# Every second wide mask on GpSimd, and ten checks at the end in thirds of a row

## The chip, the cores and the metric

The kernel runs on one core of a Trainium2 chip. Its engines work in parallel, each through its own list of instructions in a fixed order: TensorE (PE, matrix products), VectorE (DVE), ScalarE (ACT), GpSimd (POOL), and SyncE (SP), which here only starts transfers. They meet through semaphores. The metric is the device time of one execution in microseconds (us), as the median of several runs; the profile is of one further execution.

## What is computed

Four graph layers on a feature table `x` of 2708 nodes by 128 features, with one adjacency matrix `adj` of 2708 x 2708:

```python
_a = bernoulli(..., 0.00295421, (2708, 2708)); adj = _a / max(_a.sum(-1), 1)
for layer in (0, 1, 2, 3):
    h = maximum(layernorm(x), 0)
    x = x + layer(h, adj)
# layer 0: hyperbolic aggregation; layer 1: gelu messages summed over neighbours;
# layer 2: relu(adj @ (h @ W2));   layer 3: h @ W_self + (adj @ h / deg) @ W_neigh
```

A row of `adj` has some eight entries that are not zero, and all of them in a row have the same value, 1 over their number.

## The kernel before, in words

The nodes are cut into 22 tiles of 128 rows (the last has 20), and the tiles into six blocks of four (the last of two). The kernel reads `adj` transposed once, and keeps it on the chip as `mask`, one byte an element, 1 where an entry is not zero. With `mask` a product with the adjacency is a product of features with ones and zeros, and the value of each row, `val`, is multiplied in afterwards. For layer 1 it lists the neighbours of each row and gathers their feature rows from DRAM with indirect transfers, which POOL issues, tile after tile.

The work has four stretches:

- the opening (0 to about 150 us): mask, neighbour lists, layer 0;
- the loop (to about 404 us): POOL gathers, tile after tile; `messages` adds, activates and sums the gathered rows, `update` and `update_one` form the new rows of `x` and split them in three bf16 parts, and `share` multiplies the parts with the mask (layer 2's product, L2820). In gaps of the loop stand the checks of `check_part` (L2846);
- the drain after the last gather (404 to about 426 us): the last tiles' messages and updates, and the last `share`;
- the endgame (to the end): layer 2 is finished block by block (`take_two`, `times_w2`, then `one_of` for the four tiles of block 0 and `layer_two` for the other blocks), and each block's normalised rows `h` are split into a pair of fp32r parts: a rounded part by ACT (L3091, L3159) and a remainder by DVE (L3071, L3148). Layer 3's product with the adjacency is `three` (L3032): for each tile t, two parts by six blocks, twelve matmuls. Its mask operand must be fp32r too, so `widen` (L2428) copies the tile's mask, 2708 elements a row, from one byte to four, into one of five buffers; tile t uses the buffer that tile t-5 used, so it waits until that tile is multiplied (`multiplied`). Meanwhile `third_own` forms `h @ W_self` (L3176, L3180, L3185, L3200). The last five tiles are multiplied block by block, so that a block can be taken (L3318), multiplied by `W_neigh` (L997), scaled (L3325), added (L3330) and stored (L3333) while PE does the next.

The checks: that all entries of a row are one value isn't taken on trust. For every row the kernel reads `adj` again, as it lies in DRAM, counts the elements that equal `val` and later compares the count with `deg` (`wrong_rows`, L3246). If any row differs, a flag leads to a second, dense program that stands behind this one. The rows of tiles 0 to 15 (`CHECKS = 16`) are checked in the loop, in thirds of 904 columns: SP fetches, DVE compares into bytes (L2862), ACT sums (L2868). Those of tiles 16 to 21 are checked in the endgame by `check` (L3206), in halves of 1354 columns: SP fetches a whole row of the tile into one of two buffers (L3213), DVE compares and sums in one instruction (L3218).

The order of all this is written by a planner in the kernel itself (L788 to L914). Each step is entered by `op(engine, took, step, after, due, ring, filler)` with an estimated duration, the steps that it follows, a due time and, where it takes a buffer of a ring, which one; a `filler` gives way to other steps of its engine until it is due. `carry_out` then plays the plan through with these estimates and writes the instructions of each engine in the order that comes out. On the chip the order is fixed; what really takes longer than planned delays all that stands behind it on its engine.

Two points of the plan matter here. `begun_wide` (L2947) opens the first two buffers of the wide masks, so masks 0 and 1 can be made before the loop has ended. `turned` (L2981) closes the memory of the loop and opens that of the endgame; all other buffers (rows of the checks, the other masks, the pairs) exist only after it.

Of the kernel before, what the change touches and what calls it, by code (L numbers as in the profile page):

```python
# [29 lines left out]
F32 = mybir.dt.float32  # L30
# [12 lines left out]
P = 128  # L43
# [18 lines left out]
LAG = 3  # L62
WIDE = 5
MID = 1354.0
CHECKS = 16


def dense_stack(
# [491 lines left out]
def sparse_stack(  # L560
# [30 lines left out]
    def rows(t):  # L591
        return min(P, N - t * P)
# [1830 lines left out]
    wide_one, wide_mask = [], {}  # L2423

    def widening(t, after, due):
        return op("ACT", 2.47, lambda: widen(t), after, due, filler=True)

    def widen(t):  # L2428

        pool = wide_one[0] if t % WIDE < 2 else wide_one[1]  # L2430
        m = pool.tile([P, N], F32R, tag=f"wm{t % WIDE}", name=f"wm{t}")
        nc.scalar.copy(m, mask[:, t, :])  # L2432
# [4 lines left out]
    middle = -(-N // 2)  # L2437
    middle += middle % 2
    sides = ((0, middle), (middle, N))
    nb = len(blocks)  # L2440
    assert T == 22 and nb == 6 and rest

# [517 lines left out]
    def turn():  # L2960

        st_m.close()
        held.close()

        def pool(name, bufs):
            made[name] = st.enter_context(
                tc.tile_pool(name=name, bufs=bufs, reuse_waits="tile")
            )
            return made[name]

        pool("group2", 2)
        pool("block2", 2)
        wide = pool("wide2", 1)
        pool("eq", 1)
        pool("rows", 2)
        wide_one.append(pool("widemask", 1))
        made["pair"] = wide.tile([P, T, 2, D], F32R, name="pair")
        for name in ("rdeg", "clipped", "wrong", "some"):
            made[name] = wide.tile([P, T], F32, name=name)
# [223 lines left out]
        frees(s, k)  # L3203
        return k

    def check(t, due):  # L3206

        n = rows(t)
        my = {}

        def fetch():
            my["row"] = made["rows"].tile([P, N], F32, tag="row", name=f"row{t}")
            nc.sync.dma_start(out=my["row"][:n, :], in_=adj[t * P : t * P + n, :])  # L3213

        def equal(k):
            c0, c1 = sides[k]
            eq = made["eq"].tile([P, middle], F8, tag="eq", name=f"eq{t}_{k}")
            nc.vector.tensor_scalar(  # L3218
                eq[:n, : c1 - c0],
                my["row"][:n, c0:c1],  # L3220
                val[:n, t : t + 1],
                None,
                op0=ALU.is_equal,
                op1=ALU.add,
                accum_out=same[:n, t, k : k + 1],
                saturate=False,
            )

        f = op("SP", 0.1, fetch, [turned], due - 15.0, ring=("rows", 2))
        e = [  # L3230
            op("DVE", 1.65, lambda k=k: equal(k), [(f, 8.0), parts_begun], due + 1.6 * k,
               filler=True)
            for k in range(2)
        ]
        frees(f, *e)
        return e

    def inverse():
        rdeg, clipped = made["rdeg"], made["clipped"]
# [164 lines left out]
```

## Time and profile before

| | |
|---|---|
| median of 3 runs | 623.64 us (617.2 to 625.9) |
| the profiled execution, its own time | 522.63 us |
| its span, first to last instruction | 520.9 us |
| busy: PE, DVE, ACT, POOL | 431.5, 405.6, 349.4, 216.3 us |
| mean granted clock of PE | 0.90 |
| wide masks on ACT (L2432), 22 | 53.0 us busy, 2446 ns each |
| checks in the loop: DVE L2862, ACT L2868, 48 each | 685 ns (median) and 946 ns each |
| checks in the endgame: DVE L3218, 12 | 1622 ns each (median) |
| gathers on POOL in the loop (L2467) | 72 and 65, 1004 and 1032 ns each |
| POOL after the last gather, from 404.8 us | nothing |

The time of the profiled execution is its own, taken in the same way as the others; it is some 101 us below the median of the timed runs, and nothing in the profile tells why. Sums below are made against the profiled execution. A share of busy time is a mean over stretches with different limits, so each stretch is looked at by itself. In a row of groups the columns are line, engine, operation, what it writes and reads with shapes, count, busy us and mean ns, and idle time of the engine before them with what ended it. A row of the timeline has start, duration, engine, line, operation. In the chain of waits each row is start, duration and what the end of the program waited for at that moment.

### The profile page before, as it was taken

How to read it: one execution, taken by the hardware profiler on the slowest of the kernel's cores; microseconds unless marked ns; L12 is line 12 of the kernel's file. 1: busy time of each engine (PE TensorE's matmuls, PEld its weight loads, DVE VectorE, ACT ScalarE, POOL GpSimd, SP SyncE). 2: the span in 40 equal slices, each digit the busy share in tenths (PEclk: the TensorE clock that was granted, in tenths of full speed). 3: DMA queues.
4: the chain of work that ended last, by engine and by line, in shares of the span. 5: the costliest groups of instructions: out<-in, count | busy, mean ns of one | idle time of the engine just before them, and what ended most of it. 6: DMA issues, size and time to landing. Idle time of an engine off the chain costs nothing.

```text
span 520.9 us, 8318 instructions
## 1 busy us (share of the span) xinstructions
PE 431.5 (83%) x2442; PEld 295.3 (57%) x2442; DVE 405.6 (78%) x1740; ACT 349.4 (67%) x746; POOL 216.3 (42%) x270
## 2 busy tenths in 40 slices
PE   0787899999999699816789878897886898999793
PEld 0674354556557566615555646554554446888583
DVE  6888954879955895589978897999886879999432
ACT  2738965789823173465656678989787878999910
POOL 8800000000047777667777777777777000000000
PEclk9999799999999655767579997999997999999898
DMA  8893189992151111311222387769877341160012
GB/s 255 287 312 94 72 305 342 319 361 73 32 143 55 52 47 54 96 37 50 85 54 53 86 264 224 222 202 292 268 229 227 120 162 54 46 270 23 1 52 64
DMA packets 41942, 77.89 MB, mean 150 GB/s; under 512 B 5418, under 2 KB 18278, under 8 KB 41226
## 3 DMA queue, kind: packets, MB, share of 16 engines
q1 hardware_dynamic: 33582, 63.15, 35.9%
q0 software_dynamic: 6560, 13.38, 10.2%
q10 hardware_dynamic: 1744, 0.72, 0.5%
q8 instruction: 21, 0.34, 0.3%
q14 instruction: 35, 0.29, 0.2%
HBM read 73.62 MB, written 3.62 MB: 148 GB/s over the span
## 4 chain that ended last, share of the span: by engine, by line
DVE 41%; PE 23%; ACT 16%; DMA 12%; issue 6%; POOL 1%; ACTq 0%; DVEq 0%
DMA a<-in_adj_t_dram 7%; DVE eq L3218 3%; PE acc L2085 3%; PE three L3032 3%; ACT wm L2432 3%; DVE eq L2862 3%; ACT mask L1482 3%; PE u L1429 2%; ACT eq L2868 2%; DMA layer_w<-in_L_gnn_layer_dram 2%; PE msg L2535 2%; PE own L997 2%; PE own L1005 2%; PE two L2820 1%; DVE r_all L1108 1%
## 5 line engine op out<-in xcount | busy, mean ns | idle before, releaser
L2344 POOL DMA_INDIRECT early<-d_early,early_c x42 | 41.6, 990 | 134.9 <-DVE wt L1732 122.4
L2467 POOL DMA_INDIRECT g<-d_hbm,head_c x72 | 72.3, 1004 | 26.7 <-issue 16.2
L2467 POOL DMA_INDIRECT gt<-d_hbm,tail_c x65 | 67.1, 1032 | 19.8 <-issue 14.9
L2820 PE MATMUL two<-mask,parts 128*128 128x512 fp8e4 (+1 forms) x288 | 64.3, 360 | 3.3 <-ACT parts L2739 3.1
L3032 PE MATMUL three<-wm,pair 128*128 128x512 f32 (+1 forms) x264 | 62.4, 386 | 2.0 <-ACT pair L3091 1.3
L2085 PE MATMUL acc<-mask,parts 128*128 128x512 fp8e4 (+1 forms) x288 | 59.8, 362 | 2.7 <-ACT parts L1653 1.8
L3032 PEld LDWEIGHTS three<-wm,pair 128*128 128x128 f32 x264 | 47.3, 194 | 11.6 <-ACT pair L3091 1.7
L2432 ACT CAST wm<-mask 128x2708 fp32r<-128x2708 fp8e4 x22 | 53.0, 2446 | 0.0
L2868 ACT ACTIVATE eq<-eq 128x904 fp8e4<-128x904 fp8e4 (+1 forms) x48 | 45.4, 946 | 5.7 <-DVE eq L2862 5.5
L1482 ACT ACTIVATE mask<-a 128x2048 fp8e4<-128x2048 uint32 (+5 forms) x32 | 40.3, 1294 | 12.3 <-DMA a<-in_adj_t_dram 12.3
L2085 PEld LDWEIGHTS <-parts 128*128 128x128 bf16 x288 | 27.1, 100 | 32.0 <-ACT parts L1653 2.3
L2820 PEld LDWEIGHTS <-parts 128*128 128x128 bf16 x288 | 27.6, 100 | 26.8 <-ACT parts L2739 3.8
L2535 PE MATMUL msg<-rt,gt 128*128 128x128 f32 x130 | 23.1, 321 | 15.9 <-ACT gt L2613 15.7
L2535 PEld LDWEIGHTS msg<-rt,gt 128*128 128x128 f32 x130 | 19.2, 219 | 22.2 <-ACT gt L2613 21.8
L1678 PE MATMUL pk<-mask,shifts 128*128 128x512 fp8e4 (+1 forms) x132 | 28.8, 354 | 1.9 <-ACT mask L1482 1.9
L2529 PE MATMUL msg<-ident,g 128*128 128x128 f32 x144 | 25.0, 322 | 5.0 <-ACT g L2594 3.6
L2529 PEld LDWEIGHTS msg<-ident,g 128*128 128x128 f32 x144 | 21.1, 223 | 8.3 <-ACT g L2594 6.3
L2820 PE MATMUL two<-mask,partsh 128*128 128x512 fp8e4 (+1 forms) x108 | 23.3, 361 | 2.4 <-ACT partsh L2739 1.7
L2497 PEld LDWEIGHTS <-r_all 128*128 128x128 fp8e4 x195 | 15.3, 111 | 16.7 <-issue 15.3
L2497 PE MATMUL msg<-parts,r_all 128*128 128x128 bf16 x144 | 13.5, 253 | 12.3 <-DVE v L1031 10.5
L2085 PE MATMUL acc<-mask,partsh 128*128 128x512 fp8e4 (+1 forms) x108 | 21.9, 354 | 0.0
L1678 PEld LDWEIGHTS <-shifts 128*128 128x128 bf16 x132 | 12.5, 101 | 12.7 <-issue 2.0
(472 smaller groups left out, 1054.9 us busy)
## 6 DMA issues: line engine op xcount, KB each, us to landing
a<-in_adj_t_dram SPq DMA_DIRECT2D x25, 1024.0 KB
early<-in_adj_dram SPq DMA_DIRECT2D x16, 452.0 KB
hT<-in_adj_dram SPq DMA_DIRECT2D x16, 452.0 KB
row<-in_adj_dram SPq DMA_DIRECT2D x5, 1354.0 KB
early<-in_adj_dram SPq DMA_DIRECT2D x8, 450.0 KB
hT<-in_adj_dram SPq DMA_DIRECT2D x8, 450.0 KB
a<-in_adj_t_dram SPq DMA_DIRECT2D x5, 296.0 KB
a<-in_adj_t_dram SPq DMA_DIRECT2D x5, 256.0 KB
```

Of the source, the lines that this page charges most:

```text
L1482: nc.scalar.activation(to, patterns, AF.Sign, saturate=False)
L1678: nc.tensor.matmul(box["pk"][:, :w], shifts[:, t, :], mask[:, t, sl], start=(t == 0), stop=(t == T - 1),)
L2085: nc.tensor.matmul(box["acc"][:, :w], part_of(t, k), mask[:, t, sl], start=(t == 0 and k == 0), stop=(t == T - 1 and k == 2),)
L2344: nc.gpsimd.indirect_dma_start(out=to, out_offset=None, in_=d_early, in_offset=bass.IndirectOffsetOnAxis(ap=early_c[:n, t, k : k + 1], axi ...
L2432: nc.scalar.copy(m, mask[:, t, :])
L2467: nc.gpsimd.indirect_dma_start(out=g[:n, q, :], out_offset=None, in_=d_hbm, in_offset=bass.IndirectOffsetOnAxis(ap=table[:n, q : q + 1], a ...
L2497: nc.tensor.matmul(ps[:, q * D : (q + 1) * D], r_all[:, t, q * P : (q + 1) * P], part_of(t, j), start=(j == 0), stop=(j == 2),)
L2529: nc.tensor.matmul(sums(), box["g"][:n, q, :], ident[:n, :], start=False, stop=False)
L2535: nc.tensor.matmul(sums(), box["gt"][:, q, :], box["rt"][:, q, :], start=(whole(t) and q == 0), stop=(q == nq - 1),)
L2820: nc.tensor.matmul(two[b][:, : sl.stop - sl.start], part_of(t, k), mask[:, t, sl], start=(t == 0 and k == 0), stop=(t == T - 1 and k == 2),)
L2868: nc.scalar.activation(eq[0][:n, : c1 - c0], eq[0][:n, : c1 - c0], AF.Copy, accum_out=same[:n, t, k : k + 1], saturate=False,)
L3032: nc.tensor.matmul(three[b][:, : sl.stop - sl.start], made["pair"][:, t, k, :], wide_mask[t][:, sl], start=(t == 0 and k == 0), stop=(t == ...
```

## The change

It has three parts.

1. `widening` gives the odd tiles (1, 3, ..., 21, eleven of them) to POOL, with `nc.gpsimd.tensor_copy`, planned at 2.5 us, and not as fillers. The even tiles stay on ACT.
2. `CHECKS` is 12 in place of 16: the loop keeps 36 parts of checks, and the endgame gets ten tiles in place of six.
3. In the endgame these ten tiles are checked in thirds of a row, 30 parts. Each third is fetched by a transfer of its own into one of six buffers. Of each two parts one is compared by POOL (planned at 0.92 us) and then summed by ACT (0.95 us, a filler), and one is compared and summed by DVE in one instruction (1.12 us, a filler). Both write their result over the row itself, in fp32, so the buffer of byte results is gone. The parts are due 1.4 us apart from 22 us after the loop's planned end; before, whole tiles were due 4.4 us apart from 26 us on.

```diff
-CHECKS = 16
+CHECKS = 12
...
     def widening(t, after, due):
-        return op("ACT", 2.47, lambda: widen(t), after, due, filler=True)
-
-    def widen(t):
+        if t % 2:
+            return op("POOL", 2.5, lambda: widen(t, nc.gpsimd.tensor_copy), after, due)
+        return op("ACT", 2.47, lambda: widen(t, nc.scalar.copy), after, due, filler=True)
+
+    def widen(t, copy):
 
         pool = wide_one[0] if t % WIDE < 2 else wide_one[1]
         m = pool.tile([P, N], F32R, tag=f"wm{t % WIDE}", name=f"wm{t}")
-        nc.scalar.copy(m, mask[:, t, :])
+        copy(m, mask[:, t, :])
         wide_mask[t] = m
...
-        pool("eq", 1)
-        pool("rows", 2)
+        pool("rows", 6)
...
-    def check(t, due):
+    def check(t, k, due):
 
         n = rows(t)
+        c0, c1 = k * THIRD, min((k + 1) * THIRD, N)
+        apart = (3 * t + k) % 2 == 0
         my = {}
 
         def fetch():
-            my["row"] = made["rows"].tile([P, N], F32, tag="row", name=f"row{t}")
-            nc.sync.dma_start(out=my["row"][:n, :], in_=adj[t * P : t * P + n, :])
-
-        def equal(k):
-            c0, c1 = sides[k]
-            eq = made["eq"].tile([P, middle], F8, tag="eq", name=f"eq{t}_{k}")
+            my["row"] = made["rows"].tile([P, THIRD], F32, tag="row", name=f"row{t}_{k}")[
+                :n, : c1 - c0
+            ]
+            nc.sync.dma_start(out=my["row"], in_=adj[t * P : t * P + n, c0:c1])
+
+        def equal():
+            nc.gpsimd.tensor_scalar(
+                my["row"], my["row"], val[:n, t : t + 1], None, op0=ALU.is_equal
+            )
+
+        def add_up():
+            nc.scalar.activation(
+                my["row"], my["row"], AF.Copy, accum_out=same[:n, t, k : k + 1]
+            )
+
+        def both():
             nc.vector.tensor_scalar(
...
+                my["row"], my["row"], val[:n, t : t + 1], None, op0=ALU.is_equal, op1=ALU.add,
                 accum_out=same[:n, t, k : k + 1],
...
-        f = op("SP", 0.1, fetch, [turned], due - 15.0, ring=("rows", 2))
-        e = [
-            op("DVE", 1.65, lambda k=k: equal(k), [(f, 8.0), parts_begun], due + 1.6 * k,
-               filler=True)
-            for k in range(2)
-        ]
-        frees(f, *e)
-        return e
+        f = op("SP", 0.1, fetch, [turned], due - 10.0, ring=("rows", 6))
+        if apart:
+            e = op("POOL", 0.92, equal, [(f, 5.0)], due)
+            e = op("ACT", 0.95, add_up, [e], due + 1.5, filler=True)
+        else:
+            e = op("DVE", 1.12, both, [(f, 5.0), parts_begun], due, filler=True)
+        frees(f, e)
+        return [e]
...
-    for k, t in enumerate(range(CHECKS, T)):
-        equals += check(t, ended + 26.0 + 4.4 * k)
+    for k in range(3 * (T - CHECKS)):
+        equals += check(CHECKS + k // 3, k % 3, ended + 22.0 + 1.4 * k)
```

More of the change, by code (lines that the diff above doesn't have):

```diff
@@ L2436, in sparse_stack @@
     group_p = held.enter_context(tc.tile_pool(name="group", bufs=3))
-    middle = -(-N // 2)
-    middle += middle % 2
-    sides = ((0, middle), (middle, N))
     nb = len(blocks)
@@ L3204, in third_own @@
         return k
-    def check(t, due):
+    def check(t, k, due):
         n = rows(t)
+        c0, c1 = k * THIRD, min((k + 1) * THIRD, N)
+        apart = (3 * t + k) % 2 == 0
         my = {}
         def fetch():
-            my["row"] = made["rows"].tile([P, N], F32, tag="row", name=f"row{t}")
-            nc.sync.dma_start(out=my["row"][:n, :], in_=adj[t * P : t * P + n, :])
-        def equal(k):
-            c0, c1 = sides[k]
-            eq = made["eq"].tile([P, middle], F8, tag="eq", name=f"eq{t}_{k}")
[L3218 to L3224, printed above, removed]
+            my["row"] = made["rows"].tile([P, THIRD], F32, tag="row", name=f"row{t}_{k}")[
[11 more added lines that the diff above has]
+        def both():
+            nc.vector.tensor_scalar(
+                my["row"], my["row"], val[:n, t : t + 1], None, op0=ALU.is_equal, op1=ALU.add,
                 accum_out=same[:n, t, k : k + 1],
-                saturate=False,
             )
-        f = op("SP", 0.1, fetch, [turned], due - 15.0, ring=("rows", 2))
-        e = [
-            op("DVE", 1.65, lambda k=k: equal(k), [(f, 8.0), parts_begun], due + 1.6 * k,
-               filler=True)
-            for k in range(2)
-        ]
-        frees(f, *e)
-        return e
+        f = op("SP", 0.1, fetch, [turned], due - 10.0, ring=("rows", 6))
[6 more added lines that the diff above has]
+        return [e]
     def inverse():
```

## The prediction

> **What bounds the kernel now.** I read the page first, for the slices of the span, then a table of busy time by stretches of the last part, since all edits lie there, then the chain of waits from 403 us on, the groups of the endgame, and last the opening, where alone GpSimd computes. The stretch table (busy us and instructions per engine, PE, its weight loads, DVE, ACT, POOL, then the granted clock):
>
> ```profile
> 403.00:426.00 23.00, 20.11 (x109) 10.18 (x109) 20.89 (x106) 17.20 (x37) 1.22 (x2) 1.00 0.30 91
> 426.00:434.00 8.00, 6.91 (x43) 4.17 (x42) 4.56 (x28) 6.17 (x12) 0.00 (x0) 1.00 0.68 287
> 434.00:484.00 50.00, 49.66 (x271) 42.43 (x272) 47.41 (x166) 49.21 (x47) 0.00 (x0) 1.00 0.24 89
> 484.00:492.00 8.00, 4.85 (x26) 3.58 (x25) 2.85 (x12) 8.00 (x10) 0.00 (x0) 0.99 0.00 0
> 492.00:513.00 21.00, 20.37 (x111) 16.88 (x110) 8.15 (x14) 4.93 (x7) 0.00 (x0) 0.92 0.18 52
> ```
>
> Up to 404 us gathers on POOL, 1.25 us apart, pace the loop. From 404 to 426 the last tiles drain, mostly through DVE. From 434 to 484 three engines are full at once: PE 99%, DVE 95%, ACT 98%. POOL is idle. So taking work from ACT cannot move this stage by itself: PE does not wait. It waits only behind it, as the chain shows:
>
> ```profile
> 480.14 0.17 DVE nbthree L3134
> ...
> 481.99 2.34 ACT wm L2432
> 484.33 0.52 ACT pair L3159
> 484.85 2.36 ACT wm L2432
> 487.21 0.77 ACT h L3142 x2
> 487.98 2.34 ACT wm L2432
> 490.32 0.49 ACT hT L3180
> ...
> 490.85 1.23 PE self L3185 x8
> ```
>
> DVE ends layer two of block 4 at 480.3, ACT takes its rows between wide masks, and PE, which needs them, stands 0.61 us before 484.9 and 2.48 us before 490.85. That is all that a free ACT could give back after 434 us, and some 1.4 us more because the ten matmuls after that stop took 3.81 us where later tens take 2.34.
>
> **The costs of the parts.** Groups from the page and from the line of the old comparison (mean, or min/median/max, in ns):
>
> ```profile
> L2432 ACT CAST wm<-mask 128x2708 fp32r<-128x2708 fp8e4 x22 | 53.0, 2446 | 0.0
> L2868 ACT ACTIVATE eq<-eq 128x904 fp8e4<-128x904 fp8e4 (+1 forms) x48 | 45.4, 946 | 5.7 <-DVE eq L2862 5.5
> ```
>
> ```profile
> L3218 DVE TENSOR_SCALAR_CACHE_REDUCE eq<-row,val x12: 1607/1622/1631, 448.8 to 477.4; 128x1354 fp8e4<-128x1354 f32 x10, 20x1354 fp8e4<-20x1354 f32 x2
> ```
>
> (1) Twelve of the 48 checks leave the loop (tiles 12 to 15). They have the latest due times, so they are those that still run from 400 us on. On the chain between 403 and 426 us they hold DVE 0.69, 0.60, 0.60 and 0.60 us (at 403.57, 408.79, 419.31, 422.52) and ACT 1.05 us (404.28): 3.5 us. Earlier ones are hidden behind the gathers, but gathers beside a comparison are 1.37 us apart on average and the others 1.29: 12 x 0.075 = 0.9 us. Together -4.4 us. After them the wait for the last gather's rows is late next, with two small-operation chains on DVE, so no more than this.
>
> (2) Eleven wide masks leave ACT: at the 2.35 us that each holds ACT, 25.9 us off, and 15 sums of thirds come back. The page's L2868 row has 904 elements too, 1.05 us with its accumulator read: 15.8 us. Net -10 us on ACT. PE hides all but the 2.48 us at 490.85.
>
> (3) DVE's checks were 12 x 1.62 = 19.5 us; now 15 at some 1.15 us (904/1354 of 1.62 is 1.08, and every DVE operation has a fixed part) are 17.3: -2.2 us.
>
> (4) POOL gets 11 copies of 2708 elements and 15 comparisons of 904. Nothing in the trace is near in size. The nearest row is POOL's only two-sided arithmetic, L1206, 128 elements in 0.53 us. All of it taken as per-element work gives 11.1 us for a copy and 3.7 us for a comparison: the upper end. The lower end: memsets of 1 and 128 elements took 0.10 and 0.20 us, 0.84 ns an element, so a copy has 2.3 us of elements plus the 0.42 us of L1206 that is not its 128: 2.7 us. Between 434 and 490 us POOL then has ten copies and 15 comparisons. I take 1.0 ns an element, 3.1 and 1.3 us, near the lower end, for a reason that the opening shows (next part); 31 + 20 = 51 of 56 us. POOL just carries it. The copies have time: a tile's buffer is free five tiles ahead. The Trainium skill (GPSIMD Engine Reference, Engine selection) calls one-input work about line rate, which sides with the low end; the row alone, scaled, would put POOL at 166 us and the kernel beyond 600 profiled.
>
> (5) DVE shares something with a reading POOL. In the opening POOL runs L1206 without pause beside small DVE operations:
>
> ```profile
> 8.06 0.53 POOL L1206 TENSOR_SCALAR shifts<-ident 128x128 bf16<-128x128 f32 x1
> 8.13 0.24 DVE L1246 SCALAR_TENSOR_TENSOR n_an<-n_tn,n_an 128x12 f32<-128x12 f32 x1
> ...
> 9.16 0.53 POOL L1206 TENSOR_SCALAR shifts<-ident 128x128 bf16<-128x128 f32 x1
> 9.31 0.17 DVE L924 SCALAR_TENSOR_TENSOR n_qn<-n_qn 128x12 f32<-128x12 f32 x1
> ```
>
> The operation that began 0.07 us into POOL's took 0.24 us, the one 0.15 us into it 0.17 us. So DVE was held until about 0.15 us after POOL's start, while 128 elements are read: about 1.1 ns each. By these rows alone a hold costs under 0.1 us, nothing here. The Trainium skill (SBUF — State Buffer, Who interferes with whom) says more: a DVE instruction with two inputs in SBUF, or in a two-port mode, and a GpSimd instruction that reads SBUF exclude each other for the whole instruction, and accumulating comparisons are exempt. By that rule a copy holds such operations for 2.7 us and a comparison for 0.9: 10 x 2.7 + 15 x 0.9 = 40 us. Of DVE's 47 us in the full stage, checks, statistics and operations that read one input from PSUM are 29; 18 us are exposed, pair remainders, x updates and the chains of fifteen small steps. Spread at random, 40 x 18/47 = 15 us are lost; in program order DVE soon meets an exposed step within each hold, at worst losing all but some 0.55 us of each: 40 - 25 x 0.55 = 26. I take 20. This is paid on the path, because DVE has no slack there (95% busy, and block 4's rows already reach PE 0.61 us late) and its order is fixed: what waits behind the held step are the pair remainders that PE needs, and behind those ACT.
>
> (6) Copy 1 now runs on POOL right after the last gather, beside the drain: one hold, +2 us. SP issues 30 fetches instead of 6, at 0.33 us each, 10 us spread over 45 us, hidden; they start only after the turn, and no output is waiting there. But a slot of the six comes free only when the sixth part before it is summed, so a late POOL comparison delays ACT's sum (ACT waits in order, rows of x behind it), then SP, then a DVE check. By the dues in the diff the parts are 1.4 us apart, so six of them 8.4; a sum ends 2.45 us after its part's due, so a slot is free 6 us ahead of the next due, and the plan allows the fetch 5: 1 us of slack. I put 0 to 5 us on it, in the range, and 0 in the sum. The buffers and the adding of `same` cost nothing new; `wrong_rows` had 14 us before the flag is used.
>
> **The sum.** -4.4 (1) -2.5 (2) -2.2 (3) +20 (5) +2 (6) = +12.9 us. Against the profiled execution, 522.63 us with a span of 520.9: 535.5. The timed median is 623.64, 101 us above it, and the trace doesn't say why; added unchanged the gap gives 636.5, in proportion 639. I say 637. Runs of one kernel lie between 617.2 and 625.9, so 2%, 12.5 us, is about what tells a change from none.
>
> **Rivals.** Free GpSimd: holds are short, or fall on DVE's checks. Then -4.4, -3.1 and -1.4 remain, about -9: 514 profiled, 613 timed. For it: the 0.17 us rows under a busy POOL; against it: the 0.24. It decides if DVE loses under 8 us. This one ends not slower.
> Slow GpSimd: conversion from 8 bits, or a loop that costs 1.5 to 2 ns an element. At 5.4 us a copy and 2 us a comparison POOL needs 84 us for 56, +28, and holds DVE too: some +35, 658 to 665. For it: L1206's 0.53; against it: the hold's 0.15. It decides from 3.6 us a copy, where ten and 15 comparisons fill the 56 us.
> Chained waits: POOL on time on average but uneven, ACT standing before the sums: +3 to +8 on either of the first cases.
>
> **Chances.** Held DVE 0.49 (own range 625 to 652), free GpSimd 0.28, slow GpSimd 0.17, the rest 0.06 spread between. Above 636.1: half of the first, all of the slow, some of the rest: 0.48. Below 611.2: under half of the free case and a little more: 0.16. Between: 0.36. The range leaves out the fastest tenth and the slow case's upper half: 611 to 666.
>
> **What would show it.** POOL copies of 2.7 to 3.5 us. Small two-input DVE steps of 1 to 2.7 us, ending with POOL's, where 0.16 stood. PE idle before `three`, released by DVE or by ACT behind DVE. The drain after the last gather shorter by 2 to 4 us. If small steps stay at 0.16 us and PE at 99%, the free case holds; if `three` waits for POOL's copies, the slow one. Wrong altogether if the 101 us outside the profile move.

## The result, and the profile after

The changed kernel takes 637.91 us (median of 4 runs, 636.31 to 648.11), the kernel before 624.61 us in the runs beside it. The ratio is 1.0265, with a 95% interval of 1.0206 to 1.0324: slower. All ratios here compare fast runs with fast runs, and so are not the quotients of the medians beside them (here 1.0213). The prediction was 637.

The profile of before that the prediction read has a time, 522.63 us, that none of these runs has, so the first run of the experiments profiles the same kernel again; that trace (span 613.8 us, clock 0.83) is the one to set beside the changed kernel's (634.4 us, clock 0.82). By stages, from the first gather of the loop to the end of the last gather (loop), from there to the first matmul of `three` (drain), and from there to the end (endgame):

| us, one profile each | loop | drain | endgame | span |
|---|---|---|---|---|
| before, second profile | 223.8 | 46.6 | 88.1 | 613.8 |
| changed kernel | 227.5 | 51.2 | 100.5 | 634.4 |

The drain is 4.6 us longer and the endgame 12.4 us. Loops differ by some us without any change in them (222 to 230 us in the profiles from chips of this speed), so nothing is made of the 3.7 us. Drains can be told apart better: two later runs that leave the drain as it was have 46.6 and 46.9 us.

From the page of the changed kernel, the two new groups on POOL (line, engine, operation, shapes, count, busy us, mean ns, idle before):

```profile
L3218 POOL TENSOR_SCALAR row<-row,val 128x904 f32<-128x904 f32 (+2 forms) x15 | 38.9, 2605 | 24.4 <-DMA row<-in_adj_dram 20.5
L2434 POOL CAST wm<-mask 128x2708 fp32r<-128x2708 fp8e4 x11 | 26.9, 2443 | 38.0 <-PE three L3030 22.5
```

A copy of 2708 elements takes 2.44 us and a comparison of 904 takes 2.54 us (the median; 2.61 is the mean). Copies are quicker than the 3.1 us taken, comparisons twice as slow as the 1.3 us. Together POOL has 65.8 us of new work; the prediction put the comparisons and ten of the eleven copies at 51.

The same fifty-us stretch of the endgame, 4 to 6 us after the first `three`, in the changed kernel:

```profile
540.00:590.00 50.00, 41.12 (x214) 34.74 (x212) 42.41 (x117) 32.02 (x49) 37.06 (x16) 0.91 0.59 190
```

and in the second profile of before (PE, its weight loads, DVE, ACT, POOL, granted clock, DMA):

```profile
530.00:580.00 50.00, 49.14 (x268) 41.38 (x267) 45.58 (x149) 49.29 (x46) 0.00 (x0) 1.00 0.24 89
```

PE did 268 matmuls there and now does 214. ACT is rid of 17 us, as meant, and nobody is quicker for it: PE idles 9 us, and DVE, with fewer instructions, is busy almost as long. Its small steps show why. From the timeline of the changed kernel (start, duration, engine, line, operation):

```profile
565.49 2.44 POOL L2434 CAST wm<-mask 128x2708 fp32r<-128x2708 fp8e4 x1
...
566.48 1.47 DVE L928 SCALAR_TENSOR_TENSOR qthree<-rthree 128x4 f32<-128x4 f32 x1
...
567.91 2.53 POOL L3218 TENSOR_SCALAR row<-row,val 128x900 f32<-128x900 f32 x1
567.98 0.95 DVE L931 TENSOR_TENSOR qthree<-qthree,athree 128x4 f32<-128x4 f32 x1
568.97 0.16 DVE L932 SCALAR_TENSOR_TENSOR rthree<-qthree,rthree 128x4 f32<-128x4 f32 x1
```

L928 needs 0.16 us and takes 1.47: it ends at 567.95, when POOL's copy ends (567.93). L931 is held by the comparison that follows, but only 0.95 us of its 2.53; L932 runs beside the same comparison in its usual 0.16 us. I count 17 such steps from the drain on, 21.4 us above their usual durations: 14.6 beside copies, 6.8 beside comparisons; 5.5 us of them in the drain, 15.9 in the endgame.

How a held step reaches PE shows in the chain of waits:

```profile
542.13 2.35 DVE rthree L932
544.51 0.17 DVE nbthree L3132
544.71 1.65 ACT h L3140 x4
546.35 2.34 ACT wm L2434
548.69 0.48 ACT hT L3178
549.17 0.53 ACT pair L3157
549.74 2.62 PE three L3030 x6
```

L932 is held by a copy (542.01 to 544.46), ACT stands 3.94 us for the end of DVE's chain, puts a wide mask of its own between the rows and their pair, and PE stands 4.85 us before 549.74. It is the first of three long stands of PE in the endgame, 15.0 us in all; before's longest is 2.49 us.

The waits of the changed kernel from 530 us on (who waits for whom: us in total, times, longest):

```profile
ACT row L3223 <- POOL row L3218: 12.5, 7, 3.9
...
ACT h L3140 <- DVE nbthree L3132: 6.9, 3, 3.9
```

ACT stands 12.5 us before sums whose comparison POOL hasn't finished. From 557.8 to 598.5 us POOL works without a pause, and until 585.8 the chain of waits passes through it. PE's second stand, 4.42 us before 590.39, is of this kind: ACT had just waited 3.85 and 1.48 us for comparisons, and PE's rows stood behind the sums. The third is again behind held steps (timeline):

```profile
593.61 2.46 DVE L3121 TENSOR_TENSOR farthree<-halves 128x2 f32<-128x2 f32 x1
...
596.10 2.42 DVE L3123 TENSOR_TENSOR farthree<-farthree 128x2 f32<-128x2 f32 x1
...
603.52 2.08 PE L3183 MATMUL self<-self_w,hT 128*128 128x128 f32 x8 [5.76 <-DVE total L3259]
```

Two steps of 0.16 us take 2.46 and 2.42 us, beside POOL's last comparison and the copy behind it, and PE stands 5.76 us before `self`; the profile names `total`, the end of the checks, as the last to come. Each of the three stands is also followed by 4 to 5 us in which PE's granted clock is 0.50 (549 to 553, 590 to 594 and 603 to 608 us), where it is 1.00 from 534 to 544 and from 554 to 584 us. So a stand costs more than its length: PE is busy 78.2 us in this endgame, against 76.1 for the same matmuls before.

### The profile page after: what moved, and what is told of

Its sections match the earlier page's. It is cut to its first block, busy times and chain, and to the rows that moved or that the text cites. A ratio compares the mean times of both kernels' runs of the same rounds, so it can differ in the third digit from the quotient of the medians.

```text
span 634.4 us, 8390 instructions
## 1 busy us (share of the span) xinstructions
PE 460.2 (73%) x2442; PEld 314.2 (50%) x2442; DVE 417.5 (66%) x1734; ACT 330.0 (52%) x741; POOL 278.3 (44%) x296
## 4 chain that ended last, share of the span: by engine, by line
DVE 34%; PE 17%; ACT 14%; another core or an unknown queue 13%; issue 11%; DMA 7%; POOL 3%; ACTq 0%; DVEq 0%; POOLq 0%
DMA a<-in_adj_t_dram 6%; PE three L3030 3%; PE two L2819 3%; ACT eq L2867 2%; ACT mask L1482 2%; PE u L1429 2%; POOL row L3218 2%; PE msg L2534 2%; DMA layer_w<-in_L_gnn_layer_dram 2%; DVE eq L2861 1%; DVE n_s L1528 1%; ACT h L2680 1%; PE msg L2528 1%; PE msg L2544 1%
## 5 line engine op out<-in xcount | busy, mean ns | idle before, releaser
L2819 PE MATMUL two<-mask,parts 128*128 128x512 fp8e4 (+1 forms) x288 | 72.2, 390 | 6.5 <-issue 4.6
L2085 PE MATMUL acc<-mask,parts 128*128 128x512 fp8e4 (+1 forms) x288 | 63.6, 374 | 14.0 <-issue 11.2
L2085 PEld LDWEIGHTS <-parts 128*128 128x128 bf16 x288 | 29.2, 106 | 45.1 <-issue 15.0
L3218 POOL TENSOR_SCALAR row<-row,val 128x904 f32<-128x904 f32 (+2 forms) x15 | 38.9, 2605 | 24.4 <-DMA row<-in_adj_dram 20.5
L2819 PEld LDWEIGHTS <-parts 128*128 128x128 bf16 x288 | 29.9, 107 | 34.6 <-issue 13.3
L1482 ACT ACTIVATE mask<-a 128x2048 fp8e4<-128x2048 uint32 (+5 forms) x32 | 40.3, 1294 | 12.4 <-DMA a<-in_adj_t_dram 12.4
L2434 POOL CAST wm<-mask 128x2708 fp32r<-128x2708 fp8e4 x11 | 26.9, 2443 | 38.0 <-PE three L3030 22.5
L2544 PE MATMUL msg<-upd_w,aggs 128*128 128x128 f32 x44 | 13.6, 400 | 36.1 <-ACT aggs L2541 29.2
L2867 ACT ACTIVATE eq<-eq 128x904 fp8e4<-128x904 fp8e4 (+1 forms) x36 | 34.0, 946 | 3.1 <-DVE rx L927 1.8
L2544 PEld LDWEIGHTS msg<-upd_w,aggs 128*128 128x128 f32 x44 | 9.2, 253 | 43.4 <-ACT aggs L2541 34.4
L2434 ACT CAST wm<-mask 128x2708 fp32r<-128x2708 fp8e4 x11 | 26.9, 2446 | 2.1 <-PE three L3030 2.0
L2496 PEld LDWEIGHTS <-r_all 128*128 128x128 fp8e4 x195 | 18.3, 128 | 15.4 <-issue 13.9
```

Source lines behind the costliest of these rows:

```text
L1482: nc.scalar.activation(to, patterns, AF.Sign, saturate=False)
L2085: nc.tensor.matmul(box["acc"][:, :w], part_of(t, k), mask[:, t, sl], start=(t == 0 and k == 0), stop=(t == T - 1 and k == 2),)
L2544: nc.tensor.matmul(box["ps"][:, :D], box["agg"], upd_w[:, 1, :], start=True, stop=True)
L2819: nc.tensor.matmul(two[b][:, : sl.stop - sl.start], part_of(t, k), mask[:, t, sl], start=(t == 0 and k == 0), stop=(t == T - 1 and k == 2),)
L2867: nc.scalar.activation(eq[0][:n, : c1 - c0], eq[0][:n, : c1 - c0], AF.Copy, accum_out=same[:n, t, k : k + 1], saturate=False,)
L3218: nc.gpsimd.tensor_scalar(my["row"], my["row"], val[:n, t : t + 1], None, op0=ALU.is_equal)
```

## The experiments

Two theories stood against each other. **Held DVE**: a small step of DVE stops while POOL reads, and the path runs through such steps. **Overloaded POOL**: its comparisons are too slow for the endgame, and ACT, SP and the buffers wait behind it. Runs of one set share the kernel before on their chip; its median is named with each set.

### First set (before: 621.52 us)

The kernel before, unchanged.

> The kernel before, once more, for a second profile of it: the first was of an execution 101 us shorter than the timed ones. Both theories: the timed runs stay at 617 to 626 us. If the 101 us are waits that most executions have and the first profile had not, this profile has a span near 622 us, long idle stretches in the opening and the loop that no instruction of the kernel explains, as the profile after the change has, and an endgame (first matmul of three to the end) of 86 to 88 us as in the first profile. Then the endgames of the two kernels can be compared as they stand: 86.6 before, 100.5 after.

It gives 615.69 us, profiled, and 628.74 in one more run; the stages of the first are in the table above. The 522.63 us of the first profile belong to another chip, it seems: on one of the four chips of these experiments the same kernel takes 524.47 us as a median of 27 runs, on the three others 616 to 622. What the longer profile has and the short one has not are waits whose releaser the profile cannot name, in the opening and the loop (waits of the second profile of before):

```profile
DVE n_off L2027 <- remote: 29.2, 1, 29.2
DVE gt L2519 <- remote: 28.6, 3, 20.8
```

The changed kernel has the first of them at 29.3 us. The gap between chips lies ahead of `three` (434.3 us against 525.7 to the first one: 32 us in the opening, 43 in the loop, 17 in the drain); the endgame is 86.6 us in the one and 88.1 in the other. What these waits are, and whether they make the whole gap, is open.

**The masks alone.** `widening` and `widen` as changed, the checks as before:

```diff
+        if t % 2:
+            return op("POOL", 2.5, lambda: widen(t, nc.gpsimd.tensor_copy), after, due)
```

> Odd masks on GpSimd, all checks as before (16 tiles in the loop, six tiles in halves on DVE). Theory H (DVE is held by POOL's copies): in the profile after the change copies held DVE 12.3 us in all, ACT gives back 2.5 at most, so 631 to 636 us, slower than before by 1 to 2%, and single small DVE steps of up to 2.4 us that end with a copy. Theory P (POOL is overloaded by its comparisons, 2.54 us each, and ACT and SP stand behind it): POOL has 27 us of copies in 56 us and no comparison, nobody waits for it, so 618 to 625 us.

629.45 us, ratio 1.0152 (1.0085 to 1.0218); drain 51.4, endgame 93.8 us. That is 1.5 us below the held DVE's range and 4.5 above the other's. POOL has 27 us of work and mostly waits for buffers, so load can't be the reason. Eight steps are held, 13.1 us. The two in the drain, beside the copies of tiles 1 and 3 (timeline of this run):

```profile
507.32 4.83 POOL L2434 CAST wm<-mask 128x2708 fp32r<-128x2708 fp8e4 x2 [23.98 <-DVE eq L2864]
507.75 2.03 DVE L2668 TENSOR_SCALAR ax<-ssqx 128x2 f32<-128x2 f32 x1 [0.17 <-ACT jx L2656]
509.82 2.35 DVE L919 TENSOR_SCALAR rx<-ax 128x2 int32<-128x2 int32 x1
```

They stand in one tile's normalisation, one behind the other: 4.0 us above their usual 0.17, and the drain is 4.8 us longer than before's.

**The checks alone.** The changed kernel, with `widening` as it was:

```diff
-        if t % 2:
-            return op("POOL", 2.5, lambda: widen(t, nc.gpsimd.tensor_copy), after, due)
```

> All masks on ACT as before; checks as in the change (twelve tiles in the loop, ten in thirds at the end, every second third compared by GpSimd). Theory H: the comparisons alone hold DVE at most 15 x 0.95 = 14 us, in the profile after the change 9; less the 4.4 us of the loop and 2.2 of DVE: 625 to 632 us. Theory P: POOL has 38 us of comparisons in 56 us, less than it can do, so waits for it are short, but ACT, full before, has 16 us more to do: +16 less 4.4, 634 to 640 us. Both expect ACT to be the engine that PE waits for.

629.06 us, ratio 1.0141 (1.006 to 1.0221); drain 47.7, endgame 95.9 us. The time lies in the held DVE's range, but by luck: held steps are only 2.3 us, so the hold isn't the cost here. The waits of this run say what is:

```profile
POOL row L3216 <- DMA row<-in_adj_dram: 52.8, 5, 28.5
...
PE three L3028 <- ACT wm L2432: 10.0, 9, 1.9
```

POOL waits for rows and is not overloaded. ACT makes all 22 masks and 15 sums besides, and PE waits for its masks: a third cause, the added sums. The expectation had it under the overloaded POOL, though POOL's load has no part in it, and mis-sized: 16 us, where the endgame is 7.8 us longer than before's. In the full change the moved masks make room for these sums. The two halves alone cost 1.5 and 1.4%, together 2.65%.

**No comparison on POOL.** The changed kernel with

```diff
-        apart = (3 * t + k) % 2 == 0
+        apart = False
```

> The change with all 30 thirds compared and summed on DVE: POOL has only the eleven copies, ACT no sums. DVE has 15 x 1.15 = 17 us more to do. Theory H: DVE is the engine that counts, so +17 us less the 9 us that comparisons held it: 642 to 650 us, slower than the change. Theory P: POOL's and ACT's waits of the change go (ACT stood 12.5 us for comparisons), DVE's surplus goes partly into the 14 us that it was idle after 484: 628 to 636 us, faster than the change.

638.18 us, ratio 1.0267 (1.02 to 1.0335): the changed kernel's own ratio, between the two expectations. POOL holds DVE 15.5 us by copies alone, and DVE has 15 more checks of 1.15 us. Now ACT stands for DVE and not for POOL:

```profile
ACT h L3140 <- DVE nbthree L3132: 21.2, 5, 6.5
```

So in this kernel a comparison costs about the same on either engine: 2.54 us on POOL, with a hold and an ACT that waits for it, or 1.15 us on a DVE that has no room.

### Second set (before: 618.36 us)

**The masks as fills.** The masks alone, but POOL writes ones and reads nothing; the values of the odd masks are left out:

```diff
-            return op("POOL", 2.5, lambda: widen(t, nc.gpsimd.tensor_copy), after, due)
+            return op("POOL", 2.5, lambda: widen(t, lambda m, _: nc.gpsimd.memset(m.bitcast(F32), 1.0)), after, due)
```

> Only the masks are moved, as in the run with masks only, but GpSimd fills its eleven tiles with ones and reads nothing (the values of the odd masks are left out, so the sums of layer three are not the reference's). Held vector engine (GpSimd's reading is what stops DVE): no small DVE step is longer than 0.3 us beside these fills, the drain falls from 51.4 us back to 46-48, the part after it to 86-89 us, since ACT is rid of 26 us, and the time to 617-623 us. Overloaded GpSimd (it is GpSimd's 2.4 us per mask and the buffers waiting on it that cost): fills take as long as copies, so the time stays at 627-632 us.

619.86 us, ratio 1.0039 (1.0013 to 1.0064): where the held DVE put it, though the fills take 2.36 us, nearly as long as copies. So it is reading and not time on POOL that made the masks alone dear. But one line of the expectation failed. The drain is 51.7 us, no shorter than with copies, and the timeline has two held steps there:

```profile
503.35 4.67 POOL L2427 MEMSET wm<- 128x2708 f32 x2 [23.55 <-DVE eq L2864]
503.79 1.95 DVE L2668 TENSOR_SCALAR ax<-ssqx 128x2 f32<-128x2 f32 x1 [0.16 <-ACT jx L2656]
505.76 2.28 DVE L919 TENSOR_SCALAR rx<-ax 128x2 int32<-128x2 int32 x1
```

while in the endgame most steps pass a fill untouched, and one is held to its end at 542.21:

```profile
539.85 2.36 POOL L2427 MEMSET wm<- 128x2708 f32 x1 [3.18 <-PE three L3034]
...
541.22 0.16 DVE L3127 TENSOR_TENSOR farthree<-farthree 128x4 f32<-128x4 f32 x1
...
541.62 0.62 DVE L3132 TENSOR_SCALAR athree<-ssqthree 128x4 f32<-128x4 f32 x1
```

The held ones are `TENSOR_SCALAR`, with one input and an output in SBUF (the memory that the tiles lie in; matmuls put their sums in another one, PSUM); the free ones have two inputs in SBUF. I therefore counted, over the traces, every DVE step that begins within a POOL instruction (over 0.05 us after its start and over 0.35 us before its end):

| begun beside | small steps with two inputs in SBUF | small `TENSOR_SCALAR` | statistics, counting comparisons, sums with one input in PSUM |
|---|---|---|---|
| a copy (eight runs) | 21 of 21 held, to its end | 11 of 11 held | 0 of 32 held |
| a fill (this run) | 0 of 15 held | 3 of 3 held | 0 of 21 held |

Small means two or four elements a partition. Beside comparisons of 900 elements (the changed kernel, the checks alone, and the next two runs) 11 of 72 two-input steps on four elements were held, all of them begun in the first 0.53 us; all but one of the 61 others began later than 0.9 us and ran freely. The Trainium skill (SBUF — State Buffer, Who interferes with whom) draws just this table for copies and fills: two-input steps exclude only an instruction of GpSimd that reads, fast one-input forms any. The fills' gain is in the endgame: 84.7 us against 88.1, the 3.4 us that an ACT without eleven masks gives if little is held. Most of it is not the stand of 2.49 us, which is still 2.12 (ACT now stands 1.83 us for DVE's last chain): PE is busy 2.6 us less with the same matmuls, as its granted clock is at 0.50 for a shorter time (3 us against 6 or more; the last run shows what that does).

**The plan told the true duration.**

```diff
-            e = op("POOL", 0.92, equal, [(f, 5.0)], due)
+            e = op("POOL", 2.6, equal, [(f, 5.0)], due)
```

> The changed kernel with one number of the plan set to what was measured: a GpSimd comparison is planned at 2.6 us where 0.92 stood, so that the written order of ACT and DVE allows for it. The work is the same. Held vector engine: GpSimd reads as long as before and DVE is held as often, 635-642 us. Overloaded GpSimd with ACT standing before late sums: ACT's 12.5 us of waiting for GpSimd's comparisons go, 625-632 us.

630.68 us, ratio 1.0212 (1.0141 to 1.0284); drain 49.6, endgame 98.3 us. The wait that it was to remove is gone, and the time hardly moved (from the waits of this run):

```profile
ACT row L3223 <- POOL row L3218: 2.6, 2, 1.5
```

From 12.5 to 2.6 us, for half a per cent of ratio that lies within both intervals. DVE is held some 21 us, as in the changed kernel, and ACT now waits 19.9 us for DVE's `nbthree` where it waited 6.9. The time lies in the overload theory's range; but that was written from a kernel before of 621.5 us, and this chip's takes 618.4. As ratios the two ranges begin and end at 635 / 621.5 = 1.022 and 632 / 621.5 = 1.017, and 1.0212 lies just below the held DVE's and above the overload's. ACT's standing was a symptom with another wait right behind it.

**Twelve checks back in the loop.**

```diff
-CHECKS = 12
+CHECKS = 16
```

> The changed kernel, but tiles 12 to 15 stay in the loop (CHECKS 16): six tiles at the end in thirds, nine comparisons and eleven copies on GpSimd, 50 us of work where there were 66. Held vector engine: still some 15-17 us of held steps, so near the run with masks only, 626-632 us. Overloaded GpSimd: it has slack again, 619-625 us. Step (1) of the prediction: if twelve checks in the loop cost 4.4 us, loop and drain together are 4 us longer than the changed kernel's 278.7; if they cost nothing, they are equal within 2 us.

631.64 us, ratio 1.0241 (1.0177 to 1.0304): in us the upper end of the held DVE's range, as a ratio above it (632 / 621.5 = 1.017); drain 52.2, endgame 96.2 us. Loop and drain are 279.6 us, the changed kernel's 278.7: so twelve checks fewer in the loop gave the changed kernel nothing that a profile shows. POOL has 50 us of work in place of 66, with 14.5 us of waiting for rows, and the time stays; held steps are 22.8 us (17.1 by copies).

**Two masks only.** The kernel before, with

```diff
+        if t >= 20:
+            return op("POOL", 2.5, lambda: widen(t, nc.gpsimd.tensor_copy), after, due)
```

> The kernel before, with the masks of tiles 20 and 21 alone copied by GpSimd. They start behind the last small DVE steps, where PE stands 2.5 us for ACT's last transposed rows, which wait behind two wide masks. Held vector engine: hardly a DVE step is left to be held, PE's stand of 2.5 us goes, 618-621 us against 621.5. Overloaded GpSimd: two copies don't load it, so the same. If GpSimd's copies cost in another way (the time until PE sees them), no gain: 621-624 us.

619.78 us, ratio 1.0069 (1.003 to 1.0108): a loss where a gain was expected. The copy began earlier than I had placed it (timeline of this run):

```profile
572.64 2.44 POOL L2434 CAST wm<-mask 128x2708 fp32r<-128x2708 fp8e4 x1 [96.62 <-DVE rthree L919]
572.68 2.42 DVE L922 TENSOR_TENSOR qthree<-rthree 128x2 f32<-128x2 f32 x1
...
577.58 0.88 ACT L3144 ACTIVATE h<-x,nbthree,rthree 128x128 f32<-128x128 f32 x2 [1.75 <-DVE nbthree L3136]
...
578.98 0.80 PE L3187 MATMUL self<-self_w,hT 128*128 128x128 f32 x2 [3.93 <-ACT hT L3182]
```

This is the whole mechanism in four lines. One copy starts as soon as POOL may, 0.04 us before a step of DVE's last chain; that step takes 2.42 us; ACT waits 1.75 us for the chain's end, and PE stands 3.93 us where before it stood 2.49.

### Third set (before: 524.47 us) and last run (before: 616.44 us)

**Three ways to compare.** The changed kernel with each comparison of POOL cut in three:

```diff
-            nc.gpsimd.tensor_scalar(my["row"], my["row"], val[:n, t : t + 1], None, op0=ALU.is_equal)
+            nc.gpsimd.tensor_scalar(row[:, :300], row[:, :300], v, None, op0=ALU.is_equal)
+            nc.gpsimd.tensor_scalar(row[:, 300:600], row[:, 300:600], 1.0, None, op0=ALU.is_equal)
+            nc.gpsimd.tensor_tensor(
+                row[:, 600:900], row[:, 600:900], v.to_broadcast([n, 300]), op=ALU.subtract
+            )
```

> The changed kernel with each GpSimd comparison cut into three instructions of 300 elements: the first compares with a scalar per partition as before, the second with the number 1.0, the third subtracts the scalar instead of comparing, as an operation of two tensors (so the flag of wrong rows is not computed). Slow loop: all comparisons with scalars cost 0.19 us fixed and 2.67 ns an element, so 0.99 us for the first and the second. Slow scalar: the one with 1.0 takes 0.4-0.6 us, near a copy's 0.9 ns an element. Hold by reading ahead: a small DVE step beside the first is held about 0.35 us after its start, a third of the 0.95 us seen at 904 elements; hold by a fixed time: 0.95 us or whole.

The flag came out set, so the dense second program ran behind this one (9447 us in all); only the first 537 us are read. The groups of POOL in this run, from 400 to 540 us:

```profile
L3219 POOL TENSOR_SCALAR row<-row,val 128x300 f32<-128x300 f32 x14 | 15.9, 1139 | 19.0 <-ACT pair L3089 19.0
L3220 POOL TENSOR_SCALAR row<-row 128x300 f32<-128x300 f32 x14 | 13.3, 953 | 0.0
L3221 POOL TENSOR_TENSOR row<-row,val 128x300 f32<-128x300 f32 x14 | 10.0, 714 | 0.0
```

The slow loop it is, not the slow scalar: with the number 1.0 it is 0.95 us, with a scalar per partition 1.04 (median), and the subtraction of two tensors is quicker than either. From 300 to 904 elements the comparison with a scalar per partition grows from 1.04 to 2.54 us: 2.48 ns an element and 0.30 us fixed. The hold grows with the elements too:

```profile
490.63 1.04 POOL L3219 TENSOR_SCALAR row<-row,val 128x300 f32<-128x300 f32 x1
490.69 0.46 DVE L3123 TENSOR_TENSOR farthree<-farthree 128x4 f32<-128x4 f32 x1
```

The step ends 0.52 us after the comparison's start, between the two expectations; beside 900 elements (the 567.98 above) it was 1.02 us. That is 0.8 ns an element, so a comparison seems to be done with what it keeps from DVE long before its own end. One comparison does not fit: that of the last tile, on 20 partitions, held a step for its whole 2.5 us in the changed kernel (the 593.61 above), with the true duration planned (2.44 us) and with twelve checks back in the loop (2.42). In all three a copy follows it at once; in the run with the checks alone nothing follows, and the same comparison held a step only to 0.92 us. So it is the copy behind it that goes with the long hold; how is open.

**One mask, placed by the plan.** The kernel before, `if t == 20` in place of `t >= 20`, and

```diff
-        widened[t] = widening(t, [multiplied[t - WIDE]], began(t) - 4.0)
+        after = [multiplied[t - WIDE], left_of[T - 1]]
+        widened[t] = widening(t, after[: 1 + (t == 20)], began(t) - 4.0)
```

> The kernel before with the mask of tile 20 alone on GpSimd, and that copy made to wait for the last remainder of pair, so that it begins behind DVE's last small steps and not among them. Held vector engine: nothing is left to hold, PE's stand of 2.5 us ahead of self goes, the part from the first matmul of three falls from 88.1 to 85.5-87 us, 616-618 us against 618.4 (0.2-0.4%, hardly more than can be told). If a free ACT is worth nothing because DVE's rows come no earlier: 88 us, no change.

526.61 us, ratio 1.0033 (1.0018 to 1.0048): slower, and the edit didn't do what it says. A step named in the plan orders instructions of one engine; POOL had nothing queued, and no data made it wait. The copy began 0.04 us before the same L922 again, which took 2.42 us, and PE stood 3.94 us.

**Masks from tile 5 on.** The masks alone with `if t % 2 and t > 3`.

> The run with masks only, but tiles 1 and 3, whose copies fell into the drain (507.3 to 512.2 us), stay on ACT. Held vector engine: the drain falls from 51.4 to 46-48 us, since the two held steps (2.03 and 2.35 us) go; the part after it stays at 92-95 us; time 623-626 us against 629.5. If the drain was longer for another reason (another order of DVE and ACT in the plan): it stays at 50-52 us and the time at 627-631 us.

537.83 us, ratio 1.023 (1.0184 to 1.0276); drain 29.2, endgame 95.3 us. The us of the expectation were another chip's; what can be compared is the drain. The first profile of before, whose time is this chip's, has 29.8 us, and the run with three comparisons, on this chip and with copies in the drain, 33.9; so without copies the drain loses nothing, as the held DVE says. The expected gain in time did not come (ratio 1.023, against 1.0152 with all odd masks): six of the nine copies hold DVE 10.2 us and the endgame is 8.7 us longer than that profile's 86.6. The profiled execution (532.54 us) is the quickest of the five, and where the other 5 us of the median lie I can't show.

**One mask, held back by data.** The same with one line more, so that POOL can't begin before DVE's last remainder of `pair` is written:

```diff
+        if t == 20:
+            copy(m[:, :1], made["pair"][:, T - 1, 1, :1])
         copy(m, mask[:, t, :])
```

> The run with the mask of tile 20 alone, in which the copy still began among DVE's last small steps, because the plan's order alone doesn't hold back an engine whose queue is empty. Here GpSimd first copies one element per partition of the last remainder of pair into the mask's tile, so the copy of the mask can't begin before DVE has written that. Held vector engine: the same copy, some 3 us later, holds no step; L922 takes 0.16 us again where it took 2.42, PE's stand ahead of self falls from 3.9 to 2.3 us or less, the part from the first matmul of three to 85-87 us, and the time to the kernel before's or up to 2 us under it (ratio 0.996 to 1.001). If the copy costs by something other than the hold, PE's stand stays at 3.5-4 us and the ratio at 1.003.

614.3 us against 616.44, ratio 0.9942 (0.9907 to 0.9976): a gain of 0.6%, small, but its interval leaves out 1; more than the 0.996 to 1.001 expected, and the only version here that beats the kernel before. Its timeline:

```profile
573.52 0.16 DVE L922 TENSOR_TENSOR qthree<-rthree 128x2 f32<-128x2 f32 x1
...
577.96 1.16 PE L3189 MATMUL self<-self_w,hT 128*128 128x128 f32 x8 [2.09 <-ACT hT L3184]
...
578.81 0.19 POOL L2435 CAST wm<-pair 128x1 fp32r<-128x1 f32 x1 [101.70 <-DVE pair L3152]
...
579.06 2.45 POOL L2436 CAST wm<-mask 128x2708 fp32r<-128x2708 fp8e4 x1
```

The same copy, of the same length, beside no step that it can hold: L922 is 0.16 us again, PE stands 2.09 us in place of 3.9, the endgame is 84.4 us. The stand is only 0.4 us shorter than before's 2.49; most of the gain comes behind it. Six us from just after the stand, in before's second profile and in this run (PE, its weight loads, DVE, ACT, POOL, granted clock, DMA):

```profile
582.00:588.00 6.00, 5.71 (x18) 4.85 (x18) 1.12 (x2) 3.16 (x4) 0.00 (x0) 0.50 0.00 0
```

```profile
578.00:584.00 6.00, 5.66 (x33) 4.61 (x34) 1.26 (x3) 3.26 (x4) 2.63 (x2) 1.00 0.00 0
```

PE is as busy in both, with 18 matmuls in the one and 33 in the other: a matmul of `three` on 512 columns takes 0.63 us at a granted clock of 0.50 and 0.40 at 1.00. Behind 2.49 us of standing the clock was halved, behind 2.09 it was not. One pair of traces makes no rule of that (the masks alone keep 1.00 behind a stand of 2.77 us, the fills have 0.50 from 586 to 589 us behind one of 2.12), so how much of the gain another run would find is open. The runs of one mask placed badly and well settle the hold as the cause of the long stand (3.94 and 2.09 us; ratios 1.0033 and 0.9942, on different chips), with the copy's start as what differs.

## Why the prediction was right, and where not

The change is slower mainly for the reason given, steps of DVE held by a reading POOL. That the total came within 1 us is luck: some steps of the sum were wrong and offset each other.

- **(1), -4.4 us, failed.** Leaving twelve checks out of the loop gave nothing: 279.6 us of loop and drain with them, 278.7 without; the checks alone have a drain of 47.7 us against 46.6, where the prediction took 3.5 us off. The step took DVE's pieces on the chain for time that goes. It named the last gather's rows and two chains of small steps as late next, but not PE: in the drain PE's `two` is the chain's largest part (24.4% in before's second profile, with one unbroken stretch of 11.7 us at the end of the changed kernel's drain), and a check less on DVE doesn't shorten that.
- **(2), -2.5 us, holds as a size, not in the way.** With fills, which hold few steps of the endgame, it is 3.4 us shorter, but PE's stand of 2.49 us, which was to go, is still 2.12 us. The 1.4 us of ten slow matmuls behind the stand, which the prediction put beside it, are no wait for ACT: PE was busy without a gap, and in that profile its granted clock is 0.50 from 492 to 495 us (within the stretch table's 0.92). In the changed kernel the gain is hidden by the rest. That the returning sums need the room that the masks leave shows in the run with the checks alone: 10.0 us of PE waiting for ACT's masks.
- **(3), DVE's checks.** 15 of 1.15 us, 17.2 us, as worked out. Without the POOL half they are 34.5 us, and the kernel is as slow as with it.
- **(4), mis-sized in the comparison.** Copy 3.1 us taken, 2.44 measured; comparison 1.3 taken, 2.54 measured; the upper bound of 3.7 was nearer. The mistake was the split of L1206's 0.53 us: I gave 0.42 of it to the fixed part by taking a fill's 0.84 ns an element for the slope. A fill's own fixed part was in view, 0.10 us for one element, and with that L1206 gives (0.53 - 0.10) / 128 = 3.4 ns and 3.1 us a comparison, too long by a fifth (the fixed part measured is 0.30 us). The sentence of the Trainium skill on one-input work at line rate was the wrong one to lean on: it fits the copy (0.90 ns an element) and not the comparison. The same page (GPSIMD Engine Reference, Elementwise — side-by-side cycle accounting) has 4497 ns for an addition of two tensors of 2048 elements, 2.2 ns each; an estimate from that is 0.66 us for 300 elements and 2.0 us for 904. The first fits the subtraction of two tensors (0.68 us, median); the comparison, with one input, is slower than either would make it.
- **(5), 20 us of held steps, right in kind and about right in size.** 15.9 us in the endgame, for which the 20 were meant. Steps end with POOL's copies as foretold. The comparisons hold for about 1.0 us each, near the 0.9 that (5) took from a duration that was wrong: their hold isn't the instruction, as the rule of the Trainium skill would have it (SBUF — State Buffer, Who interferes with whom; that would be 15 x 2.5), but its first part. The two differences offset each other.
- **(6), +2 us in the drain, was +4.6.** The plan let both copies 1 and 3 and three comparisons begin there, not copy 1 alone, and 5.5 us of steps were held; nine copies placed elsewhere leave the drain as it was. The chained ring, put at 0 of 0 to 5, is there as 12.5 us of ACT standing; the run with the true planned duration prices it at about half a per cent, which lies within both intervals.
- **The rivals.** Free GpSimd fell. Slow GpSimd did for comparisons what it said of both, and POOL did fill up from 558 to 598 us; but relieving it, by plan or by four tiles fewer, moved little. Two of PE's three long stands are behind held steps, one behind late comparisons. So the held DVE is the larger cause, with POOL's lateness behind it.
- **The 101 us.** The profile of before was no guide to the time outside the endgame. Adding the gap unchanged was right for a reason that I did not have: it lies ahead of the endgame.

With the terms as measured the sum is 0 (1) - 3.4 (2) - 2.3 (3) + 21.4 (5 and the drain's part of 6) = +15.7 us, and up to 3 for ACT's standing. The medians differ by 13.3 us, drain and endgame of the two profiles by 17.0. This counts every held us as a us lost, which no run shows one by one; so the measured terms account for the change about as well as two single profiles allow.

## What to carry to other kernels

An idle engine isn't free capacity if its instructions hold steps of the engine on the critical path: what counts is which forms of instruction the busy engine runs while the idle one works, and here every small two-input step begun beside a copy waited for the copy's end. Before moving work, find a stretch where the other engine has nothing that can be held, and make data, not the plan's order, keep the work there: the same 2.4 us copy, begun 0.04 us before L922, cost 0.3%, and begun 5.5 us after it, gained 0.6%. And size an unknown operation from a row of its own kind, since a copy and a comparison on one engine differ threefold an element.

## What was unexpected in the hardware

- On POOL a copy with conversion from one byte to four runs at 0.90 ns an element, a comparison with a scalar at 2.48 ns plus 0.30 us, on 20 partitions as long as on 128.
- A fill, which reads nothing, still holds DVE's one-input steps with both ends in SBUF (3 of 3, to its end) and none of 15 two-input steps.
- A comparison holds two-input steps for its first 0.5 us (300 elements) or 1.0 us (900), and lets them pass for the rest, except on 20 partitions with a copy behind it.
- Behind its long stands PE ran for 4 to 6 us at a granted clock of 0.50, in the second profile of before (2.49 us of standing) and in the changed kernel (4.4 to 5.8 us), so that waiting cost it twice; not behind every stand (2.77 us with the masks alone).
- One kernel takes 524 us on one chip and 616 to 622 us on three others, with PE's granted clock at 0.89 and 0.83 (medians). The gap lies ahead of the first `three`; the slower chips' profiles have waits there that are put down to no engine.
